# Three relational graph layers: edge weights computed once and stored, stages one step apart, sums in a ring of 12 node tiles

## The chip, the cores and the metric

One NeuronCore of a Trainium2 chip runs the whole program. The metric is the device time of one execution in microseconds (us), as the median of several executions. TensorE is called PE here, VectorE DVE, ScalarE ACT, GpSimd POOL; SP issues most of the plain DMAs, POOL the gathers by index.

## The reference, cut to what matters

There are 3125 nodes with 256 features and 53,125 edges, sorted by destination. Two attention layers run first, then three relational ones. In float32:

```
x = layernorm(x + attention_2(attention_1(x)))          # two graph attention layers
h = x
for l in range(3):                                       # three relational layers
    msg = relu(h[src] * (edge_attr @ nn_w.T + nn_b))     # [53125, 256]; nn_w, nn_b are the same in every l
    out = h @ root[l] + bias[l]
    for r in range(3):                                   # edge types
        out += mean over the edges of type r at dst of msg, @ W[l, r]
    h = out
return layernorm(x + h)
```

The factor `edge_attr @ nn_w.T + nn_b` does not depend on the layer.

## The kernel before

The edges are padded to 416 tiles of 128 and worked on in 52 groups of 8 tiles; each group has two halves of 4 tiles, so a layer has 104 halves `q`. The nodes of the relational layers are cut into 25 tiles of 42, with three relations to each, that is 126 rows of sums (`KM`). The order of work is written out by hand (`manual_schedule`): each engine executes its own instructions in the order in which the Python code issues them and waits where data is missing.

`window_attention` runs the two attention layers. Beside the first one it also prepares the edge attributes for later: `attribute_rows` loads them, `turn_attributes` transposes them on PE, `store_attributes` copies them on ACT and writes them, feature by edge, to the DRAM tensor `at_d` (four DMAs a group).

`window_relational` runs the three relational layers. For each half of a group and in each layer:

- `rows` (L794) gathers `h[src]` into a tile `xsf`, one indirect DMA on POOL for 128 edges, eight for a group. The call itself stands in a helper at L382, so all gathers carry that line. There are four `xsf` buffers of a group each.
- `attributes` (L787) loads a group of turned attributes from `at_d` as `atw`; `edge_weights` (L807) multiplies them on PE with `nn_w` and leaves the product `ewf` in PSUM.
- `messages` (L816) multiplies `xsf` by `ewf` on DVE (L820: one operand in SBUF, one in PSUM), then ACT takes the relu (L821).
- `keys` (L802) builds on DVE, for a whole group, the 0/1 matrix `ohkf` that says which row of sums each edge belongs to (L804: both operands in SBUF).
- `products` (L823) multiplies `ohkf` and `xsf` on PE into `ppf`; `add` (L832) adds that on DVE to one or two places of the table `kacc` of sums (L842).
- `node` (L844), for each tile of 42 nodes once its edges are done: `means` (L854, DVE, both operands in SBUF), two transposes with copies on ACT (`turn`), two products with `W` and `root` on PE (`product`), the bias, and the DMA of the new features to the table that the next layer gathers from.

`kacc` holds all 25 node tiles. A layer's first gather waits for the last node tile of the layer before, since any edge may need it.

Of the kernel before, what the change touches and what calls it, by code (L numbers as in the profile page):

```python
# [55 lines left out]
CLEAR = 5  # L56
# [12 lines left out]
def query_blocks(g):  # L69

    return min(NT, QB + max(0, g - 2) // 2)

# [47 lines left out]
def gnn_kernel(ctx: ExitStack, tc: tile.TileContext, A, out):  # L120
# [22 lines left out]
    k_off = const.tile([1, Q4], I32, name="k_off")  # L143
# [10 lines left out]
    with tc.tile_pool(name="lk", bufs=1) as sp, tc.tile_pool(name="lkw", bufs=2) as wp, \  # L154
# [72 lines left out]
        cleared = [(CLEAR + 1 + 2 * g) * KM for g in range(NG - 1)]  # L227
# [72 lines left out]
        V.tensor_scalar(k_off, kq, float(KW), None, op0=OP.mult)  # L300
# [73 lines left out]
def sorted_edges(ctx: ExitStack, tc: tile.TileContext, A, out, L):  # L374
# [15 lines left out]
    at_d = dram.tile([DD + 1, EP], F32, name="at_d")  # L390
    L = dict(L, gather=gather, iota=iota, wid=wid, eps=eps, at_d=at_d, dram=dram)
# [5 lines left out]
    with tc.tile_pool(name="rx", bufs=1) as rx, tc.tile_pool(name="rwf", bufs=2) as wp:  # L397
        h = L["xT"].rearrange("p k n -> p (k n)")[:KM].rearrange("p (i c) -> p i c", c=D)
        acc = rx.tile([KM, KT + 2, KW], F32, name="kacc")
        rc = rx.tile([KM, KT], F32, name="rck")  # L400
        window_relational(tc, A, h_tab, out, h, acc, rc, L["nnw"], wp, L)


def window_attention(tc, A, h_tab, L):
# [8 lines left out]
    with tc.tile_pool(name="a1", bufs=1) as one, tc.tile_pool(name="kvf", bufs=6) as kp, \  # L413
# [16 lines left out]
        kvs, qws, lds, pns, ohts, qds, fs, ohs, pos, tos, abs_ = ({} for _ in range(11))  # L430
# [134 lines left out]
        def attribute_rows(g):  # L565
            ab = sp2.tile([P, G, DD], F32, name="ab")
            lo, m = g * G * P, min(G, TF - g * G)
            if m < G:
                V.memset(ab, 0.0)
                SY.dma_start(ab[:TR, m, :], A["edge_attr_32"][TF * P:, :])  # L570
            SY.dma_start(ab[:, :m, :], A["edge_attr_32"][lo:lo + m * P, :].rearrange("(t e) d -> e t d", e=P))
            abs_[g] = ab

        def turn_attributes(g):
            ab = abs_.pop(g)
            for k in range(2):
                TE.transpose(node[:, k, :], ab[:, 4 * k:4 * k + 4, :].rearrange("e t d -> e (t d)"), ident)

        def store_attributes(g):

            at = sp2.tile([P, 2, P], F32, name="atr")
            S.copy(at, node)
            for t in range(4):
                SY.dma_start(view(L["at_d"], (g * G + t) * P, [[EP, DD], [4 * P, 2], [1, P]]),
                             at[t * DD:(t + 1) * DD])

# [25 lines left out]
        for n in (1, 2):  # L612
# [34 lines left out]
            if n == 1:  # L647
                SY.dma_start(L["at_d"][DD, :].rearrange("(p c) -> p c", p=P), bc(L["ones"][:, :T // 4], 1, 4))
                attribute_rows(0)
# [3 lines left out]
            for it in range(NG + 4):  # L653
# [5 lines left out]
                if n == 1 and it + 1 < NG:  # L659
                    attribute_rows(it + 1)  # L660
# [23 lines left out]
                if n == 1 and it < NG:  # L684
                    turn_attributes(it)
                    keeps.append(lambda g=it: store_attributes(g))
# [78 lines left out]
def window_relational(tc, A, first, out, h, acc, rc, nnw, wp, L):  # L765
# [4 lines left out]
    ident, iota, gather = L["ident"], L["iota"], L["gather"]  # L770
    af = acc.rearrange("p k c -> p (k c)")

    with tc.tile_pool(name="edf", bufs=3) as sp, tc.tile_pool(name="xsf", bufs=4) as xp, \
            tc.tile_pool(name="rnf", bufs=2) as np_, \
            tc.tile_pool(name="edpf", bufs=2, space=PSUM) as ps, \
            tc.tile_pool(name="rnpf", bufs=1, space=PSUM) as ps1, tc.manual_schedule():

        def weights(n):
            w = wp.tile([P, R + 1, 2, D], F32, name="rwt")
            for r in range(R):  # L780
                SY.dma_start(w[:, r], A["L1_gnn_W"][n, r].rearrange("(k p) c -> p k c", p=P))  # L781
            SY.dma_start(w[:, R], A["L1_gnn_root"][n].rearrange("(k p) c -> p k c", p=P))
            b = wp.tile([KM, D], F32, name="rbt")
            SY.dma_start(b, A["L1_gnn_bias"][n].partition_broadcast(KM))
            return w, b

        def attributes(g):  # L787
            at = sp.tile([P, 4, P], F32, name="atw")
            av = L["at_d"][:, g * G * P:(g + 1) * G * P].rearrange("d (t k e) -> d k t e", k=2, e=P)
            for k in range(2):  # L790
                SY.dma_start(at[64 * k:64 * k + DD + 1], av[:, k])
            ats[g] = at

        def rows(n, g, table):  # L794
            xs = xp.tile([P, G, KW], F32, name="xsf")
            if n == 0:
                GP.memset(xs[:, :, D:], 1.0)
            for j in range(G):
                gather(xs[:, j, :D], table[:, :], L["src_c"][:, g * G + j:g * G + j + 1])
            xss[g] = xs  # L800
# [6 lines left out]
        def edge_weights(q):  # L807
            g, u = divmod(q, 2)
            ew = ps.tile([P, 2, 2, D], F32, name="ewf")
            for a in range(2):  # L810
                for k in range(2):
                    r = slice(64 * k, 64 * k + DD + 1)
                    TE.matmul(ew[:, k, a, :], ats[g][r, 2 * u + a, :], nnw[r, :], start=True, stop=True)  # L813
            ews[q] = ew

        def messages(q):  # L816
            g, u = divmod(q, 2)
            x4 = xss[g][:, 4 * u:4 * u + 4, :D]
            xk = x4.rearrange("p (a k) c -> p k a c", k=2)
            V.tensor_tensor(xk, xk, ews.pop(q), op=OP.mult)  # L820
            S.activation(x4, x4, AF.Relu)  # L821

        def products(n, q):  # L823
            g, u = divmod(q, 2)
            wide = D + (n == 0)
            pp = ps.tile([KM, KW], F32, name="ppf")
            for k in range(4):
                j = 4 * u + k
                TE.matmul(pp[:, :wide], ohs[g][:, j, :], xss[g][:, j, :wide], start=(k == 0), stop=(k == 3))  # L829
            pps[q] = pp  # L830

        def add(n, q):  # L832
            g, u = divmod(q, 2)
            wide = D + (n == 0)
            if u == 0:
                tos[g] = nc.values_load_multi_w_load_instructions(
                    L["k_off"][:, g * 2:g * 2 + 2], engines=[V.engine], min_val=0, max_val=(KT - 1) * KW,
                    skip_runtime_bounds_check_because="the block of a four's first dst, at most that of the padding's")[1]
            pp = pps.pop(q)
            for m, e in ((L["k_low"], 0), (L["k_high"], KW)):  # L840
                c = af[:, bass.ds(tos[g][u] + e, wide)]
                V.scalar_tensor_tensor(c, pp[:, :wide], m[:KM, q:q + 1], c, op0=OP.mult, op1=OP.add)  # L842

        def node(n, i, nxt, w, bias):  # L844

            k3 = slice(3 * i, 3 * i + 3)
            q = {}

            def means():
                if n == 0:  # L850
                    V.tensor_single_scalar(rc[:, k3], acc[:, k3, D], 1.0, op=OP.max)
                    V.reciprocal(rc[:, k3], rc[:, k3])
                q["k"] = np_.tile([KM, 3, D], F32, name="mk")
                V.tensor_tensor(q["k"], acc[:, k3, :D], bc(rc[:, k3], 2, D), op=OP.mult)  # L854
                if n < 2:
                    V.memset(acc[:, k3, :], 0.0)
# [5 lines left out]
            def turn(c):  # L862
                t = ps1.tile([P, 4 * KM], F32, name="mtf")
                for b in range(3):
                    TE.transpose(t[:, b * KM:(b + 1) * KM], q["k"][:, b, c * P:(c + 1) * P], ident[:KM, :KM])  # L865
                TE.transpose(t[:, 3 * KM:], h[:, i, c * P:(c + 1) * P], ident[:KM, :KM])  # L866
                S.copy(q["m"][:, c, :R].rearrange("p r (b k) -> p b r k", b=3),  # L867
                       t[:, :3 * KM].rearrange("p (b r k) -> p b r k", b=3, r=R))
                S.copy(q["m"][:, c, R], t[:, 3 * KM:])

            def product(c):
                if c == 0:
                    q["o"] = ps1.tile([KM, D], F32, name="opf")
                o = q["o"]
                for r in range(R + 1):
                    TE.matmul(o, q["m"][:, c, r, :], w[:, r, c, :], start=(r + c == 0), stop=(r == R and c == 1))  # L876
                if c == 0:
                    return
                V.tensor_add(h[:, i, :], o, bias)  # L879
                if n < 2:  # L880
                    SY.dma_start(nxt[i * KM:(i + 1) * KM, :], h[:, i, :])
                    return
                y = h[:, i, :]
# [3 lines left out]
                mv = np_.tile([KM, 2], F32, name="mvr")  # L887
                V.bn_aggr(mv, st)
                rs = np_.tile([KM, 1], F32, name="rsr")
                S.activation(rs, mv[:, 1:2], AF.Sqrt, bias=L["eps"][:KM])  # L890
                V.reciprocal(rs, rs)
                V.tensor_scalar(y, y, mv[:, 0:1], rs, op0=OP.subtract, op1=OP.mult)
# [3 lines left out]
            return [means, lambda: turn(0), lambda: turn(1), lambda: product(0), lambda: product(1)]  # L896

        def start(n):
            attributes(0)
            attributes(1)  # L900
            keys(0)
            edge_weights(0)
            edge_weights(1)

        ats, xss, ohs, ews, pps, tos = {}, {}, {}, {}, {}, {}
        S.memzero(acc[:, :3 * CLEAR, :])
        start(0)
        wb, table = weights(0), first
        SY.dma_start(h, first.rearrange("(i p) c -> p i c", p=KM))
        for n in range(3):  # L910
            w, b = wb
            if n < 2:
                wb = weights(n + 1)
            nxt = L["dram"].tile([NT * KM, D], F32, name=f"h_tab{n + 1}") if n < 2 else None
            steps, i = [], 0
            rows(n, 0, table)
            messages(0)
# [688 lines left out]
```

## Time and profile before

| what | value |
|---|---|
| median of 11 runs | 3169.95 us (3164.01 to 3180.77) |
| the profiled execution | 3187.29 us, span 3185.4 us |
| first attention layer, from its first gather to the first gather of the second | 105 to 758 us |
| second attention layer, to the first gather of the relational layers | 758 to 1407 us |
| first, second, third relational layer, gather to gather | 1407, 1995, 2588 us to the end |
| busy over the span | PE 78%, DVE 65%, ACT 42%, POOL 67% |
| granted PE clock, mean | 0.873 |

The page has the busy time of each engine, the span in 40 slices, the chain of waits that ended last and the costliest groups of instructions. A group is listed as line, engine, operation, output<-inputs, count, then busy us and mean ns of one, then the engine's idle time before it and what ended that. "issue" means that nothing shown held the engine. The trace behind the page can be asked for any window and any tile.

### The profile page before, as it was taken

What the parts mean: (1) busy time and instruction counts of PE and PEld (TensorE: products, weight loads), DVE (VectorE), ACT (ScalarE), POOL (GpSimd) and SP (SyncE); (2) the same over time, 40 slices, a digit from 0 to 9 for tenths busy, and PEclk for the clock granted to TensorE, in tenths of its full rate; (3) what the DMA queues carried; (4) which work ended last, traced back from release to release, by engine and by line L of the source; (5) the groups of instructions that cost most, each with busy time, mean ns of one, the idle gap of its engine ahead of it and who ended that gap; (6) DMA issues with size and microseconds to landing.
All of it is one profiled execution on the core that took longest, in us unless ns stands there. A gap on an engine that the chain in (4) does not pass through costs nothing.

```text
span 3185.4 us, 42106 instructions
## 1 busy us (share of the span) xinstructions
PE 2491.6 (78%) x12254; PEld 1832.8 (58%) x12254; DVE 2063.2 (65%) x3218; ACT 1353.2 (42%) x4284; POOL 2149.0 (67%) x2145
## 2 busy tenths in 40 slices
PE   6588888777778788757888888687888868888876
PEld 3366666654556666545666566465656646666655
DVE  4498888866888888636656555455555536566664
ACT  1097878861787777544222222122222212222222
POOL 0567777713777777227777775777777747777774
PEclk8688988888899988779989989799989888889998
DMA  3799999926888888445444442444344324444442
GB/s 104 227 259 260 263 262 259 255 81 205 244 233 237 236 231 234 124 120 146 120 114 120 115 114 84 121 117 117 112 116 118 111 80 120 118 127 118 124 118 76
DMA packets 331809, 504.99 MB, mean 159 GB/s; under 512 B 107668, under 2 KB 231987, under 8 KB 331571
## 3 DMA queue, kind: packets, MB, share of 16 engines
q0 software_dynamic: 126464, 383.52, 41.9%
q1 hardware_dynamic: 201933, 115.49, 12.8%
q10 hardware_dynamic: 3174, 3.20, 0.3%
q8 instruction: 102, 1.67, 0.2%
q14 instruction: 136, 1.11, 0.1%
HBM read 461.90 MB, written 40.10 MB: 158 GB/s over the span
## 4 chain that ended last, share of the span: by engine, by line
POOL 17%; PE 15%; issue 9%; DMA 7%; DVE 5%; SPq 1%; ACT 1%; DVEq 0%; POOLq 0%; ACTq 0%
POOL xsf L382 17%; PE ppf L829 7%; DMA xsf<-h_tab,src_c 7%; PE ewf L813 3%; PE opf L876 3%; PE mtf L865 2%; DVE kacc L842 1%; DVE mk L854 1%; DVE xsf L820 1%; SPq L781 1%; ACT xsf L821 1%; DVE ohkf L804 0%; DMA atw<-at_d 0%; PE mtf L866 0%; DVE xT L879 0%
## 5 line engine op out<-in xcount | busy, mean ns | idle before, releaser
L382 POOL DMA_INDIRECT xsf<-h_tab,src_c x1248 | 1304.7, 1045 | 432.4 <-issue 346.2
L382 POOL DMA_INDIRECT kvg<-kv_tab,src_c x832 | 836.1, 1005 | 365.1 <-issue 221.8
L829 PE MATMUL ppf<-xsf,ohkf 128*126 128x256 f32 (+1 forms) x2496 | 708.2, 434 | 141.9 <-ACT xsf L821 54.6
L498 ACT ACTIVATE kvg<-kvg,wts 128x65 f32<-128x65 f32 x3264 | 793.6, 335 | 3.5 <-DMA q_tab<-qs 0.2
L820 DVE TENSOR_TENSOR xsf<-xsf,ewf 128x1024 f32<-128x1024 f32 x312 | 380.2, 1219 | 630.3 <-DMA xsf<-h_tab,src_c 470.1
L821 ACT ACTIVATE xsf<-xsf 128x1024 f32<-128x1024 f32 x312 | 329.9, 1057 | 954.6 <-DVE xsf L820 952.3
L829 PEld LDWEIGHTS ppf<-xsf,ohkf 128*126 128x126 f32 x2496 | 522.9, 218 | 267.1 <-ACT xsf L821 88.3
L512 PE MATMUL pof<-kvg,ohn 128*128 128x260 f32 x1664 | 498.7, 465 | 160.3 <-DVE accf L523 92.8
L512 PEld LDWEIGHTS pof<-kvg,ohn 128*128 128x128 f32 x1664 | 383.1, 236 | 276.1 <-DVE accf L523 116.2
L813 PE MATMUL ewf<-nnwf,atw 33*128 33x256 f32 x2496 | 374.3, 421 | 22.5 <-DMA atw<-at_d 22.5
L471 DVE TENSOR_TENSOR kvg<-qdf,kvg 128x1024 f32<-128x1024 f32 x208 | 253.0, 1216 | 150.3 <-DMA kvg<-kv_tab,src_c 100.0
L813 PEld LDWEIGHTS ewf<-nnwf,atw 33*128 33x128 f32 x2496 | 229.5, 198 | 155.3 <-issue 83.6
L876 PE MATMUL opf<-rwt,mts 128*126 128x256 f32 x1200 | 301.9, 396 | 0.0
L876 PEld LDWEIGHTS opf<-rwt,mts 128*126 128x126 f32 x1200 | 217.9, 191 | 72.8 <-issue 46.3
L473 DVE TENSOR_REDUCE alf<-kvg 128x16 f32<-128x1024 f32 x208 | 253.8, 1220 | 7.2
L865 PE MATMUL mtf<-identf,mk 126*128 126x126 f32 x450 | 95.0, 328 | 185.3 <-DVE mk L854 182.8
L466 PE MATMUL qdf<-qw,oht 32*128 32x256 f32 x1664 | 179.8, 441 | 32.8 <-DVE kvg L471 16.4
L865 PEld LDWEIGHTS mtf<-identf,mk 126*128 126x128 f32 x450 | 53.9, 159 | 241.2 <-DVE mk L854 190.2
L804 DVE TENSOR_TENSOR ohkf<-iotas,kr_c 128x1008 f32<-128x1008 f32 x156 | 187.4, 1202 | 3.5 <-DMA h_tab<-kvg 3.5
L867 ACT COPY mts<-mtf 128x378 f32<-128x378 f32 x150 | 71.1, 474 | 276.1 <-PE mtf L866 276.1
L466 PEld LDWEIGHTS qdf<-qw,oht 32*128 32x128 f32 x1664 | 116.6, 204 | 73.1 <-issue 28.1
L842 DVE SCALAR_TENSOR_TENSOR kacc<-ppf,k_high,kacc 126x256 f32 (+1 forms) x312 | 151.3, 485 | 11.1
(200 smaller groups left out, 2017.2 us busy)
## 6 DMA issues: line engine op xcount, KB each, us to landing
atw<-at_d SPq DMA_DIRECT2D x312, 66.0 KB
xsf<-h_tab,src_c POOLq DMA_INDIRECT x1248
kvg<-kv_tab,src_c POOLq DMA_INDIRECT x832
ldb<-ld_rows SPq DMA_DIRECT2D x104, 128.0 KB
qw<-q_tab SPq DMA_DIRECT2D x416, 32.0 KB
at_d<-atr SPq DMA_DIRECT2D x208, 32.0 KB
ab<-in_edge_attr_dram SPq DMA_DIRECT2D x51, 128.0 KB
q_tab<-qs SPq DMA_DIRECT2D x50, 128.0 KB
```

The costliest lines, as they stand in the source:

```text
L382: return GP.indirect_dma_start(out=dst, out_offset=None, in_=table, in_offset=rows_of(idx))
L466: TE.matmul(qd[:, a, k, :], ohts[g][r, k, :], qws[g][r, :], start=True, stop=True)
L471: V.tensor_mul(kv, qds.pop((g, u)).rearrange("p a k c -> p (a k) c"), kv)
L473: V.tensor_reduce(al[:, t:t + 4, :], kv.rearrange("p t (h c) -> p t h c", h=H), AX.X, OP.add)
L498: S.activation(c, c, AF.Copy, scale=w[:, j * H + q:j * H + q + 1])
L512: TE.matmul(po, oh[:, j, :], kv[:, j, D:], start=(j == 0), stop=(j == G - 1))
L813: TE.matmul(ew[:, k, a, :], ats[g][r, 2 * u + a, :], nnw[r, :], start=True, stop=True)
L820: V.tensor_tensor(xk, xk, ews.pop(q), op=OP.mult)
L821: S.activation(x4, x4, AF.Relu)
L829: TE.matmul(pp[:, :wide], ohs[g][:, j, :], xss[g][:, j, :wide], start=(k == 0), stop=(k == 3))
L865: TE.transpose(t[:, b * KM:(b + 1) * KM], q["k"][:, b, c * P:(c + 1) * P], ident[:KM, :KM])
L876: TE.matmul(o, q["m"][:, c, r, :], w[:, r, c, :], start=(r + c == 0), stop=(r == R and c == 1))
```

## The change

- The first relational layer (`n == 0`) loads the raw attributes itself, transposes them on PE (`turn_attributes`), multiplies them with `nn_w`, copies the result from PSUM to a tile `ewf` in SBUF on ACT (`keep_weights`) and stores that to DRAM (`ew_d`, 104 blocks of 512 KB). The second and third layer load `ewf` from there (`load_weights`), four halves ahead. The attribute work beside the first attention layer is gone, and so is `at_d`.
- `messages` therefore multiplies `xsf` by an `ewf` in SBUF, in all three layers.
- The stages stand a step apart: in step `s`, messages of half `s`, products of half `s - 1`, sums of half `s - 3` (`LAG`). The six steps of a node tile are each a step apart too, and those left at a layer's end are sorted by kind, with a second PSUM buffer for the transposes.
- `kacc` is a ring of 12 node tiles, cleared again as each is used; the DVE looks up two places for each half instead of one.
- `xsf` becomes one tile with room for six groups, and its column of ones is written once by DVE (before: by POOL for each group of the first layer). `W` and `root` have one buffer instead of two and are loaded at a layer's start.

The core of the diff:

```diff
-        def attributes(g):
-            at = sp.tile([P, 4, P], F32, name="atw")
-            av = L["at_d"][:, g * G * P:(g + 1) * G * P].rearrange("d (t k e) -> d k t e", k=2, e=P)
-            for k in range(2):
-                SY.dma_start(at[64 * k:64 * k + DD + 1], av[:, k])
+        def turn_attributes(g):
+            t = ps1.tile([P, 4, P], F32, name="atp")
+            for a in range(4):
+                TE.transpose(t[:, a, :], ab[:, g % AB, 2 * a:2 * a + 2, :].rearrange("e k d -> e (k d)"), ident)
...
+        def keep_weights(q):
+            ew = wp.tile([P, 4, D], F32, name="ewf")
             for k in range(2):
+                S.copy(ew[:, k::2, :], ewp[:, k])
+            SY.dma_start(ew_d[q], ew.rearrange("p t c -> p (t c)"))
+            ews[q] = ew
+        def load_weights(q):
+            ew = wp.tile([P, 4, D], F32, name="ewf")
+            SY.dma_start(ew.rearrange("p t c -> p (t c)"), ew_d[q])
+            ews[q] = ew
...
         def messages(q):
             g, u = divmod(q, 2)
-            x4 = xss[g][:, 4 * u:4 * u + 4, :D]
-            xk = x4.rearrange("p (a k) c -> p k a c", k=2)
-            V.tensor_tensor(xk, xk, ews.pop(q), op=OP.mult)
+            x4 = xs[:, g % XB, 4 * u:4 * u + 4, :D]
+            V.tensor_tensor(x4, x4, ews.pop(q), op=OP.mult)
             S.activation(x4, x4, AF.Relu)
...
+            for g in range(4):
+                rows(g, table)
+            for s in range(NQ + 1):
+                g, u = divmod(s, 2)
+                if u == 0 and g + 4 < NG:
+                    rows(g + 4, table)
+                if n == 0 and s < NQ:
+                    if u == 0 and g + 2 < NG:
+                        keep_attributes(g + 2)
+                    if s + 2 < NQ:
+                        keep_weights(s + 2)
+                elif n:
+                    if s + 4 < NQ:
+                        load_weights(s + 4)
+                if s < NQ:
+                    messages(s)
+                if s:
+                    products(n, s - 1)
+                for q in range(s - LAG, s - LAG + 1 if s < NQ else NQ):
+                    if q >= 0:
+                        add(n, q)
+                if u and g + 1 < NG:
+                    keys(g + 1)
...
+            for f, _, _ in sorted(sum(parts.values(), []), key=lambda x: ((x[2] > 2) + (x[2] > 5), x[1], x[2])):
+                f()
```

## The prediction

> **What bounds the kernel now.** I read the slices of the page first, then the costliest groups, then one window per relational layer, then POOL's own waits, then the timeline around single gathers. From the page:
>
> ```profile
> POOL 0567777713777777227777775777777747777774
> ...
> L382 POOL DMA_INDIRECT xsf<-h_tab,src_c x1248 | 1304.7, 1045 | 432.4 <-issue 346.2
> ...
> L820 DVE TENSOR_TENSOR xsf<-xsf,ewf 128x1024 f32<-128x1024 f32 x312 | 380.2, 1219 | 630.3 <-DMA xsf<-h_tab,src_c 470.1
> ...
> L804 DVE TENSOR_TENSOR ohkf<-iotas,kr_c 128x1008 f32<-128x1008 f32 x156 | 187.4, 1202 | 3.5 <-DMA h_tab<-kvg 3.5
> ```
>
> POOL shows 0.7 in all steady slices, attention and relational alike, and its idle time is "issue". The message multiply waits for gathers (470 of 630 us). The windows of the three relational layers (PE, PEld, DVE, ACT, POOL busy, clock, DMA share, GB/s):
>
> ```profile
> 1404.00:1994.00 590.00, 471.25 (x2280) 344.01 (x2280) 336.86 (x490) 160.10 (x225) 437.55 (x468) 0.89 0.43 121
> 1994.00:2588.00 594.00, 476.56 (x2264) 345.46 (x2264) 327.63 (x439) 141.38 (x204) 438.70 (x416) 0.90 0.39 112
> 2588.00:3185.00 597.00, 480.35 (x2248) 351.77 (x2248) 348.57 (x538) 148.17 (x229) 435.03 (x416) 0.88 0.40 114
> ```
>
> PE's busy time (471) is larger than POOL's (438), and the chain that ended last names PE nearly as often as POOL (15% and 17%). POOL's waits in the second layer settle it:
>
> ```profile
> POOL xsf L382 <- issue: 118.5, 389, 0.3
> POOL xsf L382 <- DMA xsf<-h_tab,src_c: 2.1, 7, 0.3
> ```
>
> The longest wait is 0.3 us: every gather is followed by 0.30 us, then by the next one. POOL never stands still in a layer, so **the row of gathers is the bound**; PE keeps up. A free gather takes 0.945 + 0.305 = 1.25 us, so 416 take 520 us. The layers' gathers last 558.9, 565.1 and 561.4 us. The rest is gathers that run long, and the timeline shows beside what:
>
> ```profile
> 2712.56 0.95 POOL L382 DMA_INDIRECT xsf<-h_tab,src_c  x1 [0.30 <-issue]
> 2712.95 1.22 DVE L820 TENSOR_TENSOR xsf<-xsf,ewf 128x1024 f32<-128x1024 f32 x1 [2.86 <-DMA xsf<-h_tab,src_c]
> ...
> 2713.81 0.95 POOL L382 DMA_INDIRECT xsf<-h_tab,src_c  x1 [0.30 <-issue]
> ...
> 2715.00 1.20 DVE L804 TENSOR_TENSOR ohkf<-iotas,kr_c 128x1008 f32<-128x1008 f32 x1
> 2715.07 1.95 POOL L382 DMA_INDIRECT xsf<-h_tab,src_c  x1 [0.30 <-issue]
> ```
>
> Beside L820, which reads one operand from PSUM, the gather takes its 0.95 us. Beside L804, which reads two from SBUF, it takes 1.95 and ends 0.82 us after L804 (2717.02 against 2716.20). That holds over the trace: of 125 us by which relational gathers run long, 124 lie on gathers that overlap a DVE multiply or compare with two SBUF operands. Matching each such instruction with the gather it holds up gives 0.705 us for each of the 156 keys (L804), 0.18 for the 75 means (L854, 0.96 us long) and, in attention, 0.446 for the 104 key matrices of L505 (1.22 us, two SBUF operands). The delay follows from the phase: if the DVE instruction of 1.20 us starts x before the next gather does, that gather is 1.20 - 0.13 - x late (none above x = 1.07). Evenly spread phases over a cycle of 1.25 us make 1.07²/2/1.25 = 0.46, which is L505's row.
>
> **The change, part by part.**
>
> *Messages (312).* `ewf` moves from PSUM to SBUF, so the multiply becomes an instruction of L804's kind and length (1.20 to 1.22 us), now 104 more in each layer, all beside gathers. Lower price: most messages start when the fourth gather of their half lands, 1.95 us after its end, which puts them 0.86 us before the next gather: 0.21 each. Upper price: L804's 0.705. Between: the start phases that L820 has in this trace, put through the formula, give 0.30, 0.35 and 0.40 in the three layers, mean 0.35; spread phases give 0.446. The stored weights bring more DMA traffic, and in attention, at a DMA share of 0.8, landings scatter around 4 us instead of sitting at 1.95, so I take 0.40, between the two: 312 x 0.40 = **+125 us**. It can't be a gain, since L820 holds up nothing today.
>
> The Trainium skill (page "SBUF — State Buffer", section "Who interferes with whom") speaks on both sides of this. It infers that `tensor_tensor` takes only the read interface of the pair shared with GpSimd while descriptor generation needs the write side; by that the term would be 0 and the sum 125 us lower. It also says that a DVE instruction with two SBUF inputs and a GpSimd one that reads SBUF block each other fully, whoever starts first; by that a message could start only in the 0.30 us between gathers and would cost some 0.9 us, 281 in all, an estimate from that page. The rows differ from both: gathers do wait, and L804 is at most 0.06 us longer (1195 to 1257 ns).
>
> *Keys (156).* The same instruction, but it now follows messages and sums that wait for nobody. Ends: 0.446 (L505) and 0.705 (today); the middle, 0.575, makes **-20 us**.
>
> *Edge weights on PE.* 416 products instead of 1248: PE loses 374.3/3 = 125 us in each of layers two and three, worth nothing, since PE's cover is the gather row. In layer one PE gains 208 transposes at 0.33 us (L577, the same instruction): 68 us, or 0.65 on 4.5 us a half; 5.2 stays under POOL's new 5.6 to 5.8. ACT gains 208 copies of 128x512, between L867's 0.47 and L821's 1.06 us, say 0.6: 125 us on 160 of 590, hidden. If PE were the bound there, it would cost what the rival below says.
>
> *Stores and loads of `ewf`.* 104 blocks of 512 KB a layer add 54.5 MB in some 590 us, 92 GB/s on 112 to 121; attention runs at 260 GB/s with the same POOL pace (77% busy), so nothing on the path. They queue on SP, in order, behind the node tables' stores; loads are issued four halves (22 us) ahead, so a late one is absorbed. What they cost is scatter of landings, in the first term.
>
> *Gather waits.* In the built program nearly every gather now waits for PE too (its buffer of six groups ago). Those in front of a group wait for PE and ACT already and start after the same 0.305 us as the others. Zero. The 52 memsets that leave POOL took 0.13 us inside the gaps (0.32 instead of 0.30): zero.
>
> *Attention start.* The first gather row stalls once, because PE stood for the attributes:
>
> ```profile
> 140.21 0.29 PEld L577 LDWEIGHTS nodeps<-identf,ab 128*128 128x128 f32 x2 [12.49 <-DMA ab<-in_edge_attr_dram]
> ...
> 174.31 0.94 POOL L382 DMA_INDIRECT kvg<-kv_tab,src_c  x1 [9.26 <-ACT atr L582]
> ```
>
> Without that load PE goes on some 8 us earlier and the stall of 9.26 shrinks by as much as it can: between 3 and 9, I take **-7**. After it POOL is gapless, so the rest of the attribute work there is worth nothing.
>
> *Layer ends.* From the last gather of layer two to the first of layer three:
>
> ```profile
> 2557.92 1.97 POOL L382 DMA_INDIRECT xsf<-h_tab,src_c  x1 [0.30 <-issue]
> ...
> 2585.08 0.42 DVE L879 TENSOR_TENSOR xT<-opf,rbt 126x256 f32<-126x256 f32 x1 [6.45 <-PE opf L876]
> ...
> 2588.38 0.94 POOL L382 DMA_INDIRECT xsf<-h_tab,src_c  x1 [28.49 <-DMA atw<-at_d]
> ```
>
> Now: landing 2.7, message 1.2, relu 1.1, products 2 to 3.4, sums 1.0, two means 2.6, transposes and copies 2.4, then two tiles' products 3.7 + 5.0, the last sum 0.4 and 3.3 to the first gather: 25.4 to 26.8 instead of 28.5. With the uncertainty of PE's pace, 0 to 7: -3.5 at two ends, -3 at the program's end (35.6 us today): **-10**. Ring clearing adds 25 memsets of 0.70 us on DVE in the last layer, which is idle 40%.
>
> *Look-up.* Some eight DVE instructions on one row, at 0.15 to 0.3: **+2**. The longer start of layer one (attributes, transposes, a clearing of 36 places, which L906's 3.4 us for 15 makes 8.2) lags POOL by under 10 us, and six buffers hold 60 us of gathers: zero.
>
> Sum: 125 - 20 - 7 - 10 + 2 = +90, on the profiled 3187.3: 3277. The median of before is 0.9946 of its profiled time, so 3277 x 0.9946 = **3259 us**.
>
> **Rivals.** (1) *The messages don't hold up the gathers* (or start where it costs nothing): only the fixed -15 and the keys' 0 to -41 are left, 3131 to 3172 profiled, some 3135 by the median. It decides if a message costs under 0.11 us (35/312). For it: many of today's phases are cheap; against: all three kinds of two-operand instruction hold gathers up. (2) *Phases lock badly*: L804 itself, in the second layer, costs 0.825. At 0.705 for messages and keys: 3187 + 220 - 15 = 3392, or 3374. For it: starts are tied to landings, hence to the gather's cycle; against: the landings scatter. (3) *PE bounds layer one*: with the clock at 0.66, as in the slice from 100 to 200 us, a half takes 5.2 x 0.89/0.66 = 7.0 against 5.75: +130 on my sum, 3407, or 3388. The clock of that layer (0.89) speaks against.
>
> **How the numbers follow.** Forecast 0.77, rival 1 0.10, rival 2 0.08, rival 3 0.05. The forecast's own range: messages 0.25 with keys at 0.446 and -25 fixed make 3200, or 3183; messages 0.6 with keys unchanged and -5 make 3369, or 3351. The range given, 3185 to 3330, leaves out rivals 1 and 2 and the upper tail. A change of under 0.2% is about what a measurement of this kernel can't tell from none: faster 0.10, same 0.03, slower 0.87, where the 0.03 is the forecast's edge at 3170.
>
> **What would show it.** The mean gather rises from 1045 to some 1130 ns ((125 - 20)/1248 us); long gathers stand beside the message line; POOL's waits stay at 0.3 us; the gather row lasts 590 to 605 us a layer; PE's busy time in layers two and three falls by 125 us with no gain. I am wrong if the gathers beside messages take 0.95 us, or if POOL waits for PE or ACT in layer one.

## The result

The changed kernel takes **3303.33 us** (median of 8 runs, 3294.00 to 3310.92), the kernel before 3171.53 (31 runs, 3162.20 to 3180.77): a ratio of **1.0417** [1.0402, 1.0432], 132 us slower. The forecast had said 3259, so it was 44 us low. The profiled execution of after took 3301.09 us (span 3299.3), against 3187.29 (span 3185.4) before. The experiments ran on three chips, whose times for the kernel before differ, so each ratio below is to the kernel before on the same chip.

From the page of after (idle time and its main releaser stand last in a group's row):

```profile
POOL 0577777607777775077777775787777857777774
...
DMA 21%; PE 18%; DVE 6%; issue 5%; POOL 4%; ACT 3%; DVEq 0%; POOLq 0%; SPq 0%; ACTq 0%
...
L408 POOL DMA_INDIRECT xsf<-h_tab,src_c x1248 | 1442.8, 1156 | 534.1 <-issue 198.9
...
L843 DVE TENSOR_TENSOR xsf<-xsf,ewf 128x1024 f32<-128x1024 f32 x312 | 382.8, 1227 | 811.9 <-DMA xsf<-h_tab,src_c 758.9
...
L837 DVE TENSOR_TENSOR ohkf<-iotas,kr_c 128x1008 f32<-128x1008 f32 x156 | 186.8, 1198 | 0.0
```

The mean gather of a relational layer rises from 1045 to 1156 ns, and 1248 x 0.111 = 138 us is the whole loss and a little more. The message (L843, formerly L820) takes 1227 ns where it took 1219. The engine that does the multiply loses nothing by it; the engine beside it does. The chain that ended last now names landings of gathers (DMA, 21%) and POOL for 4%, which invites the reading that the kernel waits for transfers. POOL's own waits in the second layer contradict that (us in total, times, longest):

```profile
POOL xsf L408 <- issue: 73.7, 242, 0.3
POOL xsf L408 <- PE ppf L851: 28.0, 92, 0.3
...
POOL xsf L408 <- DMA xsf<-h_tab,src_c: 18.3, 58, 0.9
```

Inside the layer nearly every wait is at most 0.3 us (the landings' longest is 0.9; the 26.2 us before the layer's first gather are the layer's start): the gather row is still gapless and still the bound. The new releasers (the products, L851) are the waits that the prediction priced at zero. The layers by window (PE, PEld, DVE, ACT, POOL busy, clock, DMA share, GB/s):

```profile
1392.00:2022.00 630.00, 506.93 (x2472) 380.82 (x2472) 338.44 (x493) 274.83 (x465) 477.19 (x416) 0.87 0.67 201
2022.00:2665.00 643.00, 397.19 (x1432) 310.69 (x1432) 326.47 (x440) 136.73 (x204) 491.29 (x416) 0.79 0.57 177
2665.00:3299.00 634.00, 402.64 (x1432) 309.04 (x1432) 363.87 (x563) 144.11 (x229) 474.29 (x416) 0.82 0.60 182
```

PE has some 80 us less to do in layers two and three, ACT 115 more in layer one, the DMA engines are busy half as much again, and none of it sets the time: POOL's busy time alone (477, 491, 474, formerly some 437) follows the layers' length. A stretch of the timeline shows the mechanism:

```profile
2345.71 1.22 DVE L843 TENSOR_TENSOR xsf<-xsf,ewf 128x1024 f32<-128x1024 f32 x1
...
2346.12 1.63 POOL L408 DMA_INDIRECT xsf<-h_tab,src_c  x1 [0.30 <-issue]
...
2347.76 1.20 DVE L837 TENSOR_TENSOR ohkf<-iotas,kr_c 128x1008 f32<-128x1008 f32 x1
2348.05 1.72 POOL L408 DMA_INDIRECT xsf<-h_tab,src_c  x1 [0.30 <-issue]
```

Both long gathers end some 0.82 us after the DVE instruction beside them: 2346.12 + 1.63 = 2347.75 against 2345.71 + 1.22 = 2346.93; 2349.77 against 2348.96. The free gather being 0.945 us long, what a gather takes above that is called its hold-up here. Matching each gather that runs over 0.945 us with the DVE instruction that ended 0.82 us before it gives this account of the three relational layers (us of hold-up):

| held up by | before | after | per instruction, after |
|---|---|---|---|
| messages (312) | 0 | 43.1 + 45.5 + 30.5 = 119 | 0.41, 0.44, 0.29 |
| keys (156) | 110 | 40.9 + 38.3 + 37.9 = 117 | 0.79, 0.74, 0.73 |
| means (75) | 14 | 0 + 14.3 + 12.6 = 27 | 0, 0.57, 0.51 |
| gather row, length in three layers | 558.9, 565.1, 561.4 | 603.6, 618.3, 600.9 | |

The rest of the span: first gather 105.1 to 103.5; attention rows 552.5 to 543.7 and 545.4 to 544.8; the spaces after them 0.8 shorter; layer ends 29.1 to 26.2 and 28.5 to 24.6; program end 35.6 to 30.6. With the relational rows' +137.4 that makes +113.8, the difference of the spans.

### The profile page after: what moved, and what is told of

It is laid out like the page before. It is cut to its first block, busy times and chain, and to the rows that moved or that the text cites. A ratio compares the mean times of both kernels' runs of the same rounds, so it can differ in the third digit from the quotient of the medians.

```text
span 3299.3 us, 40315 instructions
## 1 busy us (share of the span) xinstructions
PE 2358.0 (71%) x10694; PEld 1781.9 (54%) x10694; DVE 2081.3 (63%) x3255; ACT 1446.7 (44%) x4472; POOL 2280.1 (69%) x2093
## 3 DMA queue, kind: packets, MB, share of 16 engines
q10 hardware_dynamic: 3174, 3.20, 0.3%
## 4 chain that ended last, share of the span: by engine, by line
DMA 21%; PE 18%; DVE 6%; issue 5%; POOL 4%; ACT 3%; DVEq 0%; POOLq 0%; SPq 0%; ACTq 0%
DMA xsf<-h_tab,src_c 20%; PE ppf L851 11%; POOL xsf L408 4%; DVE xsf L843 4%; PE opf L902 4%; ACT xsf L844 3%; PE ewp L817 2%; DMA xT<-h_tab 1%; DVE kacc L865 1%; PE atp L804 0%; DMA abf<-in_edge_attr_dram 0%; DVE mk L878 0%; PE mtf L891 0%; PE ppf L902 0%; DVEq L843 0%
## 5 line engine op out<-in xcount | busy, mean ns | idle before, releaser
L408 POOL DMA_INDIRECT xsf<-h_tab,src_c x1248 | 1442.8, 1156 | 534.1 <-issue 198.9
L851 PE MATMUL ppf<-xsf,ohkf 128*126 128x256 f32 (+1 forms) x2496 | 805.1, 479 | 545.1 <-ACT xsf L844 544.4
L851 PEld LDWEIGHTS ppf<-xsf,ohkf 128*126 128x126 f32 x2496 | 563.5, 236 | 723.7 <-ACT xsf L844 620.0
L843 DVE TENSOR_TENSOR xsf<-xsf,ewf 128x1024 f32<-128x1024 f32 x312 | 382.8, 1227 | 811.9 <-DMA xsf<-h_tab,src_c 758.9
L902 PEld LDWEIGHTS opf<-rwt,mts 128*126 128x126 f32 x1152 | 247.9, 215 | 50.6 <-DVE xT L906 3.1
L488 PE MATMUL qdf<-qw,oht 32*128 32x256 f32 x1664 | 191.6, 439 | 31.6 <-DMA qw<-q_tab 15.9
L516 ACT ACTIVATE wts<-soft 128x32 f32<-128x32 f32 x104 | 20.4, 196 | 352.7 <-PE soft L514 352.4
L865 DVE SCALAR_TENSOR_TENSOR kacc<-ppf,k_low,kacc 126x256 f32 (+1 forms) x312 | 149.3, 479 | 2.5 <-PE ppf L851 0.9
L817 PE MATMUL ewp<-nnwf,atw 33*128 33x256 f32 x832 | 122.0, 413 | 9.8 <-ACT ewf L822 9.8
L822 ACT COPY ewf<-ewp 128x512 f32<-128x512 f32 x208 | 112.4, 598 | 32.6 <-PE ewp L817 32.4
L527 DVE TENSOR_TENSOR ohn<-iotas,nr_c 128x1024 f32<-128x1024 f32 x104 | 126.6, 1217 | 0.0
```

The lines of the kernel that those rows point to most:

```text
L408: return GP.indirect_dma_start(out=dst, out_offset=None, in_=table, in_offset=rows_of(idx))
L488: TE.matmul(qd[:, a, k, :], ohts[g][r, k, :], qws[g][r, :], start=True, stop=True)
L817: TE.matmul(ewp[:, k, a, :], ats[g][r, 2 * u + a, :], nnw[r, :], start=True, stop=True)
L843: V.tensor_tensor(x4, x4, ews.pop(q), op=OP.mult)
L851: TE.matmul(pp[:, :wide], ohs[g][:, j, :], xs[:, g % XB, j, :wide], start=(j == 4 * u), stop=(j == 4 * u + 3))
L902: TE.matmul(q["o"], q["m"][:, c, r, :], w[:, r, c, :], start=(r + c == 0), stop=(r == R and c == 1))
```

## Experiments

The theory: a DVE instruction with two SBUF operands holds up the gather that starts beside it, so the messages cost time because their weights moved from PSUM to SBUF, and the keys cost time in both kernels. The rivals: the stored weights' DMA traffic slows the gathers; the gathers are slowed by the changed order of work; and, for the remedies, that PE or a landing becomes late as soon as POOL is freed. The first four ran on one chip (before there: 3173.81), the next four on another (3191.8), the last ones on a third (3703.49 and 3694.71).

**1. Messages from PSUM again, traffic kept** (changed kernel).

```diff
-V.tensor_tensor(x4, x4, ews.pop(q), op=OP.mult)
+w4 = ews.pop(q)
+if n: w4 = ewp.rearrange("p k a c -> p (k a) c")
+V.tensor_tensor(x4, x4, w4, op=OP.mult)
```

> The changed kernel, but in the second and third relational layer the message multiply reads its second operand from PSUM (the place of the last computed weights) instead of the loaded tile in SBUF, so those layers use wrong weights; the loads of the stored weights still run, with nobody reading them. Theory (the gathers wait for a DVE instruction with two operands in SBUF): the 76 us that messages hold up gathers in these two layers (45.5 + 30.5) go, 3303 - 76 = 3227 us, give or take 20 for shifted phases of the keys; the message line stands beside gathers of 0.95 us. Rival (the stored weights' DMA traffic and the later landings slow the kernel): nothing of that traffic is gone, 3290 to 3315 us.

Layers two and three so multiply by wrong weights; only the time counts here. Measured 3181.32 (3173.12 to 3188.03), ratio 1.0021 [1.0002, 1.0041]: below even the theory's range.

```profile
L408 POOL DMA_INDIRECT xsf<-h_tab,src_c x1248 | 1322.4, 1060 | 537.0 <-issue 204.9
...
L846 DVE TENSOR_TENSOR xsf<-xsf,ewp 128x1024 f32<-128x1024 f32 x208 | 252.8, 1216 | 435.6 <-DMA xsf<-h_tab,src_c 434.2
```

The gather rows are 598.1 us in the unedited first layer and 558.5 and 546.2 in the two edited ones. In the timeline, a gather that starts inside such a message:

```profile
2305.76 1.22 DVE L846 TENSOR_TENSOR xsf<-xsf,ewp 128x1024 f32<-128x1024 f32 x1 [4.38 <-DMA xsf<-h_tab,src_c]
...
2305.91 0.94 POOL L408 DMA_INDIRECT xsf<-h_tab,src_c  x1 [0.30 <-DMA xsf<-h_tab,src_c]
```

It takes 0.94 us, and so do the others: of the 205 gathers in these two layers that start inside such a message none takes over 0.96 us. The stores and loads ran as before, so the traffic rival is refuted. The gain is larger than the theory's figure because the keys and means in the two layers also fell, from 103 to 64 us: they moved to other phases.

**2. Only the operand's place, in the kernel before** (no DMA added; ACT copies the weights to SBUF).

```diff
+es = np_.tile([P, 2, 2, D], F32, name="ews")
+S.copy(es.rearrange("p k a c -> p (k a c)"), ew.rearrange("p k a c -> p (k a c)"))
-ews[q] = ew
+ews[q] = es
```

> The kernel before, with one thing added: ACT copies each half's edge weights from PSUM to a tile in SBUF, and the message multiply reads that. No DMA is added. Theory: 312 messages at 0.35 to 0.45 us of held-up gather each, +110 to +140, so 3280 to 3310 us from 3172. Rival (DMA traffic): no more than 10 us from the extra copy's latency, 3165 to 3185 us.

Measured 3320.33 (3315.80 to 3324.36), ratio 1.0460 [1.0420, 1.0500].

```profile
L382 POOL DMA_INDIRECT xsf<-h_tab,src_c x1248 | 1446.4, 1159 | 430.7 <-issue 341.7
...
L822 DVE TENSOR_TENSOR xsf<-xsf,ews 128x1024 f32<-128x1024 f32 x312 | 382.4, 1226 | 808.1 <-DMA xsf<-h_tab,src_c 765.1
```

The mean gather is 1159 ns, as in the changed kernel (1156), and the split is the same: messages 117, keys 119, means 30. One operand's move from PSUM to SBUF brings the whole loss; sequence, ring and traffic are not needed for it. (ACT's copies are new here too; in layers two and three of experiment 1 and of the changed kernel ACT makes none, and the hold-up goes and comes with the operand all the same.)

**3. The same lever on the keys, in the kernel before**: row numbers and reciprocal counts are kept in the free half of a PSUM bank that is held anyway.

```diff
+bank = ps1.tile([P, 512], F32, name="opf")
+iota_p, rc = bank[:, D:D + KM], bank[:KM, D + KM:D + KM + KT]
+V.tensor_copy(iota_p, iota[:, :KM])
-V.tensor_tensor(oh, bc(iota[:, :KM], 1, G), ...)
+V.tensor_tensor(oh, bc(iota_p, 1, G), ...)
-q["o"] = ps1.tile([KM, D], F32, name="opf")
+q["o"] = bank[:KM, :D]
```

> The kernel before, with the row numbers that the keys compare with, and the reciprocal counts of the means, kept in PSUM in the relational layers, so that neither instruction has two operands in SBUF. Theory: the 124 us of long gathers (110 beside the keys, 14 beside the means) go, 3172 - 124 = 3048 us, if PE keeps up with a half each 5.0 us; where it doesn't, up to 3100. All relational gathers take 0.95 us. Rival (the keys are only late when the gathers are late for another reason): 3160 to 3180 us.

Measured 3069.57 (3068.59 to 3073.71), ratio **0.9673** [0.9637, 0.9708].

```profile
L382 POOL DMA_INDIRECT xsf<-h_tab,src_c x1248 | 1180.9, 946 | 430.1 <-issue 335.9
...
L804 DVE TENSOR_TENSOR ohkf<-opf,kr_c 128x1008 f32<-128x1008 f32 x156 | 186.9, 1198 | 3.5 <-DMA h_tab<-kvg 3.5
```

The mean gather takes 946 ns (the longest 1.13 us) and the rows are 521.3, 519.6 and 520.5 us: the free 520. The program's end grew from 35.6 to 49.5 us (the nodes' work now ends that much later after the last gather), which takes back 14 of the 124 us that left the three rows; with small differences elsewhere the profiled execution gained 114 us. By the medians the gain is 104, as the profiled execution of before lies above its median (see below).

**4. The same on the changed kernel.** The edit is that of 3.

> The changed kernel with the same step: row numbers and reciprocal counts in PSUM, messages still from SBUF. Theory: the 117 us beside the keys and 27 or more beside the means go, the 119 beside the messages stay, within 30 as their phases shift: 3303 - 145 = 3158 us, 3130 to 3190. Rival (DMA traffic): 3290 to 3315 us.

Measured 3235.35 (3224.74 to 3242.92), ratio 1.0204 [1.0165, 1.0243].

```profile
L408 POOL DMA_INDIRECT xsf<-h_tab,src_c x1248 | 1367.2, 1096 | 537.0 <-issue 196.2
```

Keys and means hold up nothing, as they should, but the messages now cost 61.3, 63.1 and 62.8 us: 187 instead of 119, or 0.59 to 0.61 each. Half of the gain went back. This is a miss for the theory's number (3130 to 3190 expected), not its mechanism: **the hold-ups don't add**, since removing one kind shifts where in the gather's cycle the other kind starts.

**5. Row numbers in PSUM in attention too** (kernel 3 and this).

```diff
-node = ps1.tile([P, 2, P], F32, name="nodeps")
+bank = ps1.tile([P, 4, P], F32, name="nodeps")
+node, iota_p = bank[:, :2, :], bank[:, 2, :]
+V.tensor_copy(iota_p, iota)
```

> The kernel before with row numbers and reciprocal counts in PSUM in the relational layers, and the attention layers' row numbers in PSUM too. Theory: beside the 104 us that the relational part alone brought, the 47 us of long gathers in the two attention layers (L505) go: 3070 - 47 = 3023 us. Rival: attention runs at 230 to 260 GB/s, so there the DMAs are nearly the bound and the gain is given back: 3060 to 3070 us.

Measured 3086.44 (3062.35 to 3094.29), ratio 0.9675 [0.9642, 0.9707]: no better than 3. The profiled execution, 3062.35, was the fastest of the four. In it the hold-ups left the attention rows too (the second lasted 523.5 us, 545.5 in kernel 3), but in the first POOL now stands still for some 43 us (12 in kernel 3), and the row lasts 565.2 us (555.6). POOL's waits in that stretch:

```profile
POOL kvg L382 <- issue: 154.9, 368, 9.8
```

The wait of 9.8 us is the stall that the kernel before has too (9.26 us at 174 us). New are the shorter ones, up to 3.2 us: 28 of them, nearly all in front of a group of eight gathers, where kernel 3 has two. So something else in that stretch falls behind as soon as the gathers take 0.95 us; "issue" doesn't say what.

**6. The attribute work four groups later** (kernel 5 and this), to test the cause that the prediction gave for the first row's stall.

```diff
-attribute_rows(0)
-if n == 1 and it + 1 < NG: attribute_rows(it + 1)
+if n == 1 and 0 <= it - 3 < NG: attribute_rows(it - 3)
-if n == 1 and it < NG: turn_attributes(it) ...
+if n == 1 and 0 <= it - 4 < NG: turn_attributes(it - 4) ...
```

> As the last one, and the attribute work beside the first attention layer starts four groups later, so that PE doesn't stand for the first attribute load. Theory (the gain that the change has at the start of attention is that stand): the stall of 9 us in the first gather row goes, 3023 - 9 = 3014 us. Rival (the stall has another cause): as the last one.

Measured 3089.69 (3087.02 to 3099.77), ratio 0.9685 [0.9654, 0.9716]. The stall is still there. What PE and POOL waited for:

```profile
178.49 0.66 PE L578 MATMUL nodeps<-identf,ab 128*128 128x128 f32 x2 [14.00 <-DMA ab<-in_edge_attr_dram]
...
187.60 0.94 POOL L382 DMA_INDIRECT kvg<-kv_tab,src_c  x1 [11.58 <-PE soft L479]
```

This doesn't refute the cause, since the edit moved the load together with the transposes that need it: PE still stands for the first attribute load, 14.00 us here (12.49 before). But the stand now ends at 178.5 us instead of 140.2, and POOL's stall at 187.6 instead of 174.3. The stall followed the stand, which speaks for the cause that the prediction gave. A kernel that turns the attributes after their load has long landed was not run.

**7. The message in four pieces** (changed kernel; weights stay in SBUF).

```diff
-V.tensor_tensor(x4, x4, ews.pop(q), op=OP.mult)
+w4 = ews.pop(q)
+for c in range(4):
+    V.tensor_tensor(x4[:, c, :], x4[:, c, :], w4[:, c, :], op=OP.mult)
```

> The changed kernel with each message multiply in four instructions of 256 columns instead of one of 1024. Theory: a gather is held up until the one DVE instruction that is running ends, so its length counts: by the phase formula (0.42 - 0.13) squared / 2 / 1.25, times four, makes 0.135 us for a message instead of 0.38, 42 us instead of 119; keys and means stay: 3303 - 77 = 3226 us, 3200 to 3260. Rival (what counts is how long DVE reads two SBUF operands altogether, 1.7 us instead of 1.2): 3303 to 3350 us.

Measured 3161.71 (3149.39 to 3174.04), ratio 0.9916 [0.9891, 0.9941].

```profile
L408 POOL DMA_INDIRECT xsf<-h_tab,src_c x1248 | 1291.3, 1035 | 536.6 <-issue 154.5
...
L845 DVE TENSOR_TENSOR xsf<-xsf,ewf 128x256 f32<-128x256 f32 x1248 | 482.2, 421 | 530.7 <-DMA xsf<-h_tab,src_c 495.0
```

The same work takes DVE 482 instead of 383 us and the program some 5% less. With pieces of 0.42 us the phase formula gives (0.42 - 0.13)²/2/1.25 = 0.034 us a piece; measured were 23 us for 1248, or 0.02. The keys fell with them, from 117 to 66 us, which the theory had not counted, so the time lies below its range. This smallest remedy alone brings the changed kernel level with the one before, or 0.8% ahead.

**8. Keys from PSUM and messages in four** (4 and 7 together).

> Both steps on the changed kernel: row numbers and reciprocal counts in PSUM, messages in four instructions. Theory: of the 188 us that messages cost with the keys in PSUM some 42 stay: 3235 - 146 = 3090 us, 3060 to 3120. Rival: 3235 to 3280 us.

Measured 3091.48 (3087.73 to 3099.12), ratio 0.9688 [0.9659, 0.9718]. The mean gather is 980 ns and the messages' hold-up 39 us, against 187 in experiment 4 with the same keys: the two-operand messages were what was left there.

**9. All steps together** (8 and the attention edit of 5), run twice.

> The changed kernel with row numbers and reciprocal counts in PSUM, messages in four instructions, and the attention layers' row numbers in PSUM as well. Theory: the 22 us of long gathers in each attention layer go, as they did in the second one of the kernel before (545 to 523 us); with no attribute work beside the first one it can follow: 0.969 of the kernel before becomes 0.955. Rival (attention is bound by its DMAs or buffers as soon as POOL is quicker, as the first one was): 0.960 to 0.970.

> The same kernel as e9_all_steps, which ran where the kernel before took 3703 us at a granted clock of 0.80 and POOL stood waiting. Theory: where the kernel before takes about 3170 to 3190 us at a clock near 0.87, gathers bound all five layers, and the ratio is 0.955; rival (attention gives its gain back to other waits): 0.960 to 0.970. Where the clock is again near 0.80: 0.98, as then.

Measured 3635.96, ratio 0.9798 [0.9767, 0.9830], and 3636.88, ratio 0.9835 [0.9781, 0.9889]. On this chip the kernel before takes 3703.49 us and PE is granted a lower clock (0.79 to 0.80 over the span of this kernel, 0.80 for the kernel before there, 0.87 in the profile of before). The long gathers are nearly gone (11, 17 and 14 us a layer), but POOL now waits 62 to 81 us in each relational layer and some 136 in each attention row. So it doesn't tell whether all steps would beat kernel 3 on the first chips; that stays open.

**10. The keys in four pieces, in the kernel before**, on the same chip.

```diff
-V.tensor_tensor(oh, bc(iota[:, :KM], 1, G), ...)
+for j in range(0, G, 2):
+    V.tensor_tensor(oh[:, j:j + 2, :], bc(iota[:, :KM], 1, 2), ...)
```

> The kernel before with each keys instruction in four of 252 columns, both operands still in SBUF. Theory (the length of one instruction counts): the keys' 110 us become some 10 to 25, by the four-piece messages' 0.02 us a piece: 0.970 of the kernel before. Rival (the total time with two SBUF operands counts): 1.00.

Measured 3713.20, ratio 1.0030 [0.9999, 1.0062]: no gain. That is the rival's number, but not its reason: the keys' hold-ups fell as the theory has it, from 65.9 us (in the next run) to 15.6, but gathers were not the bound.

**11. The kernel before, unchanged, on that chip.**

> The kernel before, unchanged, for a second profile. Its first profiled execution took 3187 us where the median was 3172. If the difference is in how the keys' phases fall, the long gathers make less than 125 us here and the time is near 3172 or the chip's own median; if it is a fixed cost of the profile, gathers make 125 us again and the time is some 15 us above the chip's median.

3704.92 us. POOL's waits in the second layer, and, from the page, the chain of work that ended last over the whole run:

```profile
POOL xsf L382 <- issue: 178.8, 389, 11.3
...
PE 31%; issue 8%; another core or an unknown queue 6%; DVE 5%; POOL 3%; DMA 1%; ACT 1%; DVEq 0%; ACTq 0%; SPq 0%; POOLq 0%
```

The same row of waits is 118.5 us with a longest of 0.3 in the profile of before, and the chain there has POOL 17% and PE 15%. There POOL never stood still in that layer; here it stands for up to 11.3 us, so gathers are not the bound, and that is why 9 and 10 gain less. That PE binds instead, at its clock of 0.80, is what the chain suggests, but it is not shown: PE is busy for a smaller share of the span (72% against 78%), and around the longest wait it shows almost no work from 2360 to 2386 us, at a granted clock of 0.50. What held it there stays open.

## Why the prediction came out as it did

*Sign and mechanism: right.* Gathers beside L843 run long, POOL's waits stay at 0.3 us, the rows last 601 to 618 us (590 to 605 forecast), PE's lighter load brings nothing. Experiments 1 and 2 show the mechanism from both sides.

*Messages: right, +119 for +125.* The middle of the bounds, 0.40 each, was 0.38 in the trace. That it came so near is partly luck: the layers lie at 0.41, 0.44 and 0.29, and it is a number of this schedule, 0.59 to 0.61 in experiment 4.

*Keys: the step that failed in kind.* I took a middle value on the ground that keys would follow work that waits for nobody, and booked -20; they cost +7, at 0.75 each. In the trace of after 129 of the 154 keys inside the gather rows stand right behind a message that waited for a landing and its two sums, and 144 of the 154 start 0.25 to 0.5 us before the next gather, 0.29 in the median (2347.76 against 2348.05 above). The message itself sets this: the gather that it holds up ends 0.82 us after it, the next one starts 0.30 us later, and the keys start 0.83 us after the message's end, so 0.29 before that gather. The prediction's own formula makes 1.07 - 0.29 = 0.78 of it. Where messages hold up nothing, in layers two and three of experiment 1, the medians are 0.60 and 0.63 and the keys cost 52 us instead of 76; in experiment 2, in the old order of work, it is 0.29 again. So keys and messages were not two terms that could be priced apart. That is rival 2's mechanism, on the keys alone. It cost 27 us of the sum.

*Means: not priced, +13.* The matching behind the prediction had 0.18 for each of the 75 means, and no term was made of it, though the change moves them too; they became 0.51 to 0.57 in two layers. An instruction that already holds up gathers needs a term whenever its neighbours move.

*Attention start: the amount was near, the cause supported.* The first row lost 8.8 us for the 7 forecast, and the first gather came 1.6 earlier instead of 2 later. I had blamed PE's wait for the first attribute load. After has neither that stand nor the stall, and in experiment 6 the stall moved with the stand. Whether the load alone makes it, or the rest of the attribute work too, no run separates.

*Layer ends: right,* -11.8 for -10. *Edge weights on PE, ACT's copies, stores and loads, gather waits: right at zero* in time, with layer one's PE at 507 us in 630 and no wait of POOL's over 0.32 us inside that layer's row. Only PE's relief was smaller than the 125 us forecast (477 to 397, 480 to 403): its granted clock was 0.79 and 0.82 in these layers, formerly 0.90 and 0.88, and a product of L851 took 479 ns where L829 had taken 434.

*From profile to median: failed.* I scaled 3277 by 0.9946, because the profiled execution of before (3187.29) was that much above its median. In fact it lies above all 31 timed runs of before, while the profiled 3301.09 of after lies amid its own; without the factor the forecast would have been 3277. That took 18 us off. It is no fixed cost of being profiled: in experiment 11 the profiled execution took 3704.92 beside a median of 3703.49. Why that one took longer was not found; the chips differ by as much (3174 to 3192), and the record doesn't say on which one it ran.

Together in profiled time: keys 27, means 13, messages -6, attention -7, ends -2, smaller ones -1, which makes the 24 us between 3277 and 3301.

The rule on the shared pair that the prediction weighed (the Trainium skill, page "SBUF — State Buffer", section "Who interferes with whom") meets the measurements thus: its inference that `tensor_tensor` leaves descriptor generation alone would make experiment 2's ratio 1, and 1.046 was measured; of its mutual exclusion between a DVE instruction with two SBUF inputs and a GpSimd one that reads SBUF one half is seen, as the gathers wait, and the other is not: it would stretch the messages too, and L843 takes 1227 ns beside L820's 1219. Here the gather alone pays.

## What to carry to other kernels

When a row of indirect gathers is the bound, price every DVE instruction beside it by where its operands lie: a big one with two SBUF operands can cost that row a quarter to two thirds of its own length (0.29 to 0.79 of some 1.2 us here), one with an operand in PSUM costs nothing, and four short pieces cost far less than one long piece. Moving data from PSUM to SBUF to spare another engine is then no saving, and a constant operand in a spare corner of a PSUM bank is one (3.3% here). Don't add such hold-ups up one by one: they depend on phase, so removing one kind can raise another (119 to 187 us), and an instruction that holds up a gather also sets the phase of what stands behind it (the keys at 0.29 us). A freed bound ends where the next one stands, as experiments 5 and 9 show.

## What the hardware showed that I had not expected

- The hold-up has a fixed tail: a gather that was held up ends 0.82 us after the DVE instruction, close to its whole free 0.945 us, while the DVE instruction gets at most some 0.08 us longer (1.30 us in experiment 4, where the median is 1.225).
- Landings got slower with no wait of POOL's over 0.9 us behind it: where a message starts on the landing of its half's fourth gather, that landing comes 2.27, 3.54 and 3.69 us (medians of the three layers) after the gather's end, 1.97, 1.96 and 1.95 before, with 201, 177 and 182 GB/s instead of 112 to 121. The layer with the most traffic has the smallest rise, so what slows them is open.
- The same kernel took 3172 to 3192 us on some chips and 3704 on another, which granted PE a clock of 0.80; there gathers are not the bound, and the remedies tried there bring less (0.98 for all steps together, 1.003 for experiment 10).
